# Turning a short chunk of tokens as a full one, with other banks, other engines and one store in place of four, in a masked attention kernel

## The chip, the cores and the metric

The kernel runs on one core of one Trainium2 chip. The metric is device time in microseconds (us) for one execution; the median of three runs is quoted. All data are float32. The core has TensorE (PE, with its weight loads shown as PEld), VectorE (DVE), ScalarE (ACT), GpSimd (POOL) and SyncE (SP), which issues transfers. TensorE writes its results to PSUM, here eight banks of 128 partitions by 512 float32; VectorE and ScalarE empty them.

## The reference

The input x has 8 batches of 512 features by 1024 tokens, cond_2048 is a mask of 0 and 1 for every token, Wq and Wo are 512 by 512.

```python
xt = transpose(x, (0, 2, 1))
q = xt @ Wq.T                                  # 8 heads of 64
scores = scale * einsum('bhqd,bhkd->bhqk', qh, qh)
logits = (scores * cmask + (1 - cmask) * NEG) * rmask
attn = softmax(logits, axis=-1)
ctx = einsum('bhqk,bhkd->bhqd', attn, qh)      # values are the queries too
x + transpose(ctx @ Wo.T, (0, 2, 1))
```

Queries, keys and values are the same projection. A masked key has no weight. A masked query has equal logits everywhere, so its context is the mean over all tokens, and all masked queries of a batch share one result.

## The kernel before, in words

About half the tokens are masked, so the kernel computes with the kept tokens alone, padded to a fixed number NK of 544 columns, of which the last stands for the masked queries and holds the mean token. It finds the kept tokens' places, writes the tokens row by row to a table in DRAM (`xd`), gathers the kept rows, and works on those. If a batch had more kept tokens than fit, or a denominator came out too small, other paths would run; in the execution profiled here they don't.

The 544 columns are five chunks: four of 128 and a short one of 32 (`sizes`, `LAST`, `END`). Heads go in pairs of 64 + 64 rows, so a batch is four pairs, and `pairs` is the list of all 32. For each pair the main loop in `late` goes over five steps (k = 0 to 4, in the order short chunk, then the four full ones), and each step computes the scores of one chunk (`scores`, L687 and L709; the exponentials on ScalarE at L695 and L712). Around the scores the loop does the work that `slots_of` has put into that step: the weighted sums of the pair before (`go_on_attend`, `end_attend`, L751), the values and their lengths of the next pair (`turn_values`, `copy_values`, `lengths_of`, `bias_of`), the projection of the pair after that (`project`, L601), and in some pairs the tokens of the next batch and the output products of the batch before. The order of instructions on each engine is exactly the order in which these functions are called; there is no scheduler.

The parts that the change touches:

- `collect` (L553) turns one chunk of gathered tokens (`xin`, tokens by features) into features by tokens: four turns by TensorE into one PSUM bank, then one copy into `xc`. A full chunk, and all chunks of batch 0, use a transpose (L560). The short chunk of later batches multiplies by the first 32 columns of the identity (L562). Its `xin` holds 128 gathered rows.
- `put_mean` (L569) makes the mean column. Its product shares a bank with the output of the short chunk and with one chunk of the values; VectorE copies it out at L585.
- `bank` hands out PSUM banks. The tag "t" has two banks, "a" has two, and the remaining four belong to the scores. The "a" banks hold the running weighted sums of a pair, from the end of its last step until `end_attend` in step 2 of the next pair (copied out by ScalarE at L778).
- In the third pair of a batch (`new` in `slots_of`), step 3 calls `collect` for five chunks, then `lengths_of`, two of the seven half products of the output (`product`, L968: the output projection is done with seven products of half size in place of eight), and the projections for the first pair of the next batch. Batch 0 does its stage in a branch of its own (`late` in `slots_of`).
- `lengths_of` (L642) squares the values (ScalarE, L646), sums them by head (VectorE, L648) and takes their maximum (L655); TensorE turns it (L658) for a bound on the scores.
- `end_output` (L1040) finishes the output of the last batch: a product with the last pair, added to partial sums by VectorE (L1050, L1057), then stored into the table `od` in DRAM. The short chunk has its 512 features in four groups of 32 partitions, and is stored by four transfers, two from SP and two from ACT (L1060). `fetch_last` (L1090) then gathers eight times from `od`; the first gather waits for chunk 0's and the short chunk's stores. `finish_tokens` (L1119 to L1121) turns the gathered rows, adds x and stores the result.

Of the kernel before, what the change touches and what calls it, by code (L numbers as in the profile page):

```python
# [12 lines left out]
AF = mybir.ActivationFunctionType  # L13
ALU = mybir.AluOpType
# [292 lines left out]
def attention_of_kept_tokens(ctx, tc, n, x, mask, wq, wo, out, ident, wqT, woT, verdict, flag):  # L307


    nc = tc.nc  # L310
    B, D, T = x.shape
    P = 128
# [16 lines left out]
    sizes, places = [], []  # L329
# [40 lines left out]
    def bank(name, tag="t"):  # L370
        if shared["all"]:
            shared["n"] += 1
            tag = "ta"[shared["n"] % 2]
        return ps.tile([P, NB], F32, tag=tag, name=name, bufs=2)
# [3 lines left out]
    xs, xbars, xmeans, xds, xins, xcs, parts, searches = {}, {}, {}, {}, {}, {}, {}, {}  # L378
# [172 lines left out]
        xins[b].append(xin)  # L551

    def collect(b, i, copy=None, tag="t"):  # L553
        n = sizes[i]
        xin = xins[b][i]
        pt = bank(f"xc_{b}_{i}", tag)
        for d in range(ND):
            to, cols = pt[:, d * n : (d + 1) * n], slice(d * P, (d + 1) * P)
            if n == P or b == 0:
                nc.tensor.transpose(to, xin[:n, cols], ident[:n, :n])  # L560
            else:
                nc.tensor.matmul(to, xin[:, cols], ident[:, :n], start=True, stop=True)  # L562
        m = min(n, NK - 1 - i * P)
        (copy or nc.scalar.copy)(
            xcs[b][:, :, i * P : i * P + m],
            pt[:, : ND * n].rearrange("p (d n) -> p d n", d=ND)[:, :, :m],
        )
# [22 lines left out]
    qTs, vs, tops, biases = {}, {}, {}, {}  # L590
# [48 lines left out]
        turn_values(pair)  # L639
        copy_values(pair)  # L640

    def lengths_of(pair):  # L642

        nm = "%d_%d" % pair
        sq = sb.tile([P, NC, P], F32, tag="sq", name=f"sq_{nm}", bufs=1)
        nc.scalar.activation(sq, vs[pair], AF.Square)  # L646
        lengths = sb.tile([P, 2 * NC], F32, tag="len", name=f"len_{nm}")
        nc.vector.tensor_reduce(  # L648
            lengths,
            sq.rearrange("p c (h d) -> p (c h) d", h=2),  # L650
            axis=AX.X,
            op=ALU.add,
        )
        tops[pair] = sb.tile([P, 1], F32, tag="top", name=f"top_{nm}")
        nc.vector.tensor_reduce(tops[pair], lengths, axis=AX.X, op=ALU.max)  # L655
# [218 lines left out]
    ods, gs, xrs = {}, {}, {}  # L874
# [68 lines left out]
            else:  # L943
                nc.vector.tensor_tensor(to, late_[:, upper], both["s", 2][:, j, :], ALU.subtract)

    def product(b, i):

        def tokens(j, m):
            cols = slice(m * P, (m + 1) * P)
            if i in (3, 5, 6, 7):  # L950
                return both["s", {3: 4, 5: 1, 6: 2, 7: 3}[i]][:, j, cols]
            first = 2 * P if i == 4 else 0
            cols = slice(first + m * P, first + (m + 1) * P)
            return cTs[b, j if i == 1 else 2 + j][:, cols]

        def features(j):
            if i == 1:
                return woT[:, j, 0:HALF]
            if i == 2:
                return woT[:, 2 + j, 0:HALF]  # L960
            if i == 3:
                return woT[:, 2 + j, HALF:D]
            return both["t", {4: 4, 5: 1, 6: 2, 7: 3}[i]][:, j, :]

        po = bank(f"po_{b}_{i}")
        for m in range(2):
            for j in range(2):
                nc.tensor.matmul(  # L968
                    po[:, m * HALF : (m + 1) * HALF],
                    tokens(j, m),  # L970
                    features(j),
                    start=(j == 0),
                    stop=(j == 1),
                )

        def new(name):
            t = both[name] = sb.tile([P, D], F32, tag="oc", name=f"{name}_{b}", bufs=LAST)
            return t

        def store(t, row, col):  # L980
            rows = slice(END + row * 2 * P, END + (row + 1) * 2 * P)
            nc.gpsimd.dma_start(  # L982
                ods[b][rows, col * HALF : (col + 1) * HALF].rearrange("(m p) c -> p m c", p=P),
                t.rearrange("p (m c) -> p m c", m=2),
            )

        add = nc.vector.tensor_tensor
        if i == 1:
            ods[b] = dr.tile([NK, D], F32, tag="od", name=f"od_{b}")
            nc.scalar.copy(new("c11"), po)  # L990
        elif i == 6:
            add(new("c12"), po, both["c11"], ALU.add)  # L992
        elif i == 7:
            add(new("c21"), po, both["c12"], ALU.add)
        elif i == 5:
            add(new("c22"), po, both["c21"], ALU.add)
            add(both["c12"], po, both["c12"], ALU.add)
            store(both["c22"], 1, 1)
        elif i == 2:
            add(both["c11"], po, both["c11"], ALU.add)  # L1000
            store(both["c11"], 0, 0)
        elif i == 3:
            add(both["c12"], po, both["c12"], ALU.add)
            store(both["c12"], 0, 1)
        else:
            add(both["c21"], both["c21"], po, ALU.subtract)  # L1006
            store(both["c21"], 1, 0)
# [32 lines left out]
    def end_output(b, i):  # L1040
        n = sizes[i]
        parts = P // n
        w = D // parts
        if i == 0:
            ods[b] = dr.tile([NK, D], F32, tag="od", name=f"od_{b}")
        po = bank(f"po_{b}_{i}")
        add_product(b, i, ND - 1, po, True, True)
        oc = new_rows(b, i, w)
        if parts == 1:
            nc.vector.tensor_tensor(  # L1050
                oc.rearrange("p (d a f) -> p a d f", d=ND, a=A),
                po.rearrange("p (a d f) -> p a d f", d=ND, a=A),
                partials[i].rearrange("p (a d f) -> p a d f", d=ND, a=A),
                ALU.add,
            )
        else:
            nc.vector.tensor_tensor(oc[:, :w], po[:, :w], partials[i][:, :w], ALU.add)  # L1057
        for k in range(parts):
            queue = nc.scalar if k % 2 else nc.sync
            queue.dma_start(ods[b][places[i], k * w : (k + 1) * w], oc[k * n : (k + 1) * n, :w])  # L1060

    def in_blocks(t):
        return t.rearrange("(k f) (a n) -> a f k n", f=Q, a=A)
# [71 lines left out]
    def slots_of(p):  # L1135

        b, pr = pairs[p]
        todo = [[] for _ in range(NC)]
        before = pairs[p - 1] if 0 < p < len(pairs) - 1 else None
        behind = pairs[p + 1] if p + 1 < len(pairs) else None  # L1140
        ahead = pairs[p + 2] if p + 2 < len(pairs) else None

        def do(k, f, *args):
            todo[k].append(lambda: f(*args))
# [3 lines left out]
        by_vector = nc.vector.tensor_copy  # L1148
# [36 lines left out]
        halves = ()  # L1185
# [5 lines left out]
        if not new:  # L1191
            if halves and pr == 1:
                leads[p] = [lambda: product(b - 1, 1)]
                halves = halves[1:]
# [6 lines left out]
        if p == 0:  # L1201
            do(0, project, behind, 1)
            do(1, values, behind)
            do(1, lengths_of, behind)
            do(1, project, ahead, 0)
            do(2, project, ahead, 1)
            do(3, bias_of, behind)
        elif late:
            do(1, values, behind)
            do(2, lengths_of, behind)  # L1210
            do(2, end_attend, before)
            do(2, put_mean, b + 1)
            do(2, collect, b + 1, 0)
            do(3, bias_of, behind)
            do(3, collect, b + 1, 1, by_vector, "a")
            do(3, collect, b + 1, 2, None, "a")
            do(4, collect, b + 1, 3)
            do(4, collect, b + 1, 4)
            for hf in range(2):
                do(4, project, ahead, hf, None, "a")  # L1220
        elif new:
            do(1, short_with_values if halves else mean_with_values)
            do(2, end_attend, before)
            do(3, collect, b + 1, 0, by_vector)
            do(3, collect, b + 1, 1, by_vector)
            do(3, collect, b + 1, 2, by_vector, "a")
            do(3, collect, b + 1, 3, None, "a")
            do(3, collect, b + 1, 4, by_vector)
            do(3, lengths_of, behind)
            for i in halves:  # L1230
                do(3, product, b - 1, i)
            for i in due:
                do(3, output, b - 1, i)
            do(3, project_with_top, 0)
            do(3, project, ahead, 1, None, "a")
        elif ahead:
            do(1, project_with_values)
            do(2, lengths_of, behind)
            do(2, end_attend, before)
            if pr == 1 and b + 1 == B and in_halves:  # L1240
                for k, i in ((2, 1), (2, 6), (3, 7), (3, 5), (4, 2), (4, 3), (4, 4)):
                    do(k, product, b - 1, i)
            do(3, project_with_top, 1, "a" if halves and pr == 1 else "t")
        elif behind:
            do(1, values, behind)
            do(2, lengths_of, behind)
            do(2, end_attend, before)
            do(3, bias_of, behind)
        if p == ND - 1:
# [428 lines left out]
```

## Time and profile before

| | |
|---|---|
| median of three runs | 630.98 us (630.52 to 632.31) |
| the profiled execution | 632.33 us, of which 630.5 us lie between its first and last instruction (the span) |
| busy in the span | PE 597.7, DVE 411.2, ACT 367.0, POOL 223.5 us |
| turns of full chunks, L560 | 128 of 128x128, 17.1 us busy |
| turns of short chunks, L562 | 56 records, 6.8 us busy |
| moved by DMA | 118.02 MB, 187 GB/s in the mean |

The rows of the groups read as: source line, engine, operation, the tile written and the tiles read, shapes, count; then busy time and, where given, the idle time before them with what ended it. A row of the timeline begins with the start in us from the start of the span and the length in us; equal instructions that follow each other are merged into one row with their count. A full-precision matmul stands as two records, a transpose as one. Records overlap, as matmuls are pipelined, so the time that a group holds TensorE is best taken from its start to the start of the next group. A wait's row reads: who waited, for whom, us in total, how often, the longest.

### The profile page before, as it was taken

How to read it: one execution, taken by the hardware profiler on the slowest of the kernel's cores; microseconds unless marked ns; L12 is line 12 of the kernel's file. 1: busy time of each engine (PE TensorE's matmuls, PEld its weight loads, DVE VectorE, ACT ScalarE, POOL GpSimd, SP SyncE). 2: the span in 40 equal slices, each digit the busy share in tenths (PEclk: the TensorE clock that was granted, in tenths of full speed). 3: DMA queues.
4: the chain of work that ended last, by engine and by line, in shares of the span. 5: the costliest groups of instructions: out<-in, count | busy, mean ns of one | idle time of the engine just before them, and what ended most of it. 6: DMA issues, size and time to landing. Idle time of an engine off the chain costs nothing. (4 is left out here: it accounts for less than half of the span.)

```text
span 630.5 us, 16440 instructions
## 1 busy us (share of the span) xinstructions
PE 597.7 (95%) x6298; PEld 416.8 (66%) x6298; DVE 411.2 (65%) x1139; ACT 367.0 (58%) x983; POOL 223.5 (35%) x317
## 2 busy tenths in 40 slices
PE   4799999999999999999999999999999999999963
PEld 3666676677667766777667766777667766765432
DVE  6539767556567767777577767777568735854542
ACT  4256758754766567754776477753775467536400
POOL 6530403232075304731164304830274305337031
PEclk7699999999999999999999999999999999999985
DMA  7565444354488668987698678978695654878557
GB/s 230 181 232 143 143 161 112 107 207 157 150 189 220 215 220 202 193 246 238 192 186 224 211 222 188 204 228 254 183 188 148 171 182 95 172 264 138 114 174 206
DMA packets 95025, 118.02 MB, mean 187 GB/s; under 512 B 11959, under 2 KB 61815, under 8 KB 94942
## 3 DMA queue, kind: packets, MB, share of 16 engines
q1 hardware_dynamic: 74078, 75.17, 39.9%
q0 software_dynamic: 16544, 39.63, 27.1%
q10 hardware_dynamic: 4320, 2.13, 1.2%
q8 instruction: 50, 0.82, 0.5%
q14 instruction: 33, 0.27, 0.2%
HBM read 74.19 MB, written 42.70 MB: 185 GB/s over the span
## 5 line engine op out<-in xcount | busy, mean ns | idle before, releaser
L695 ACT ACTIVATE e<-s,bias 128x544 f32<-128x544 f32 x256 | 180.4, 709 | 70.6 <-PE s L687 67.7
L687 PE MATMUL s<-qT 64*64 64x272 f32 x2048 | 148.6, 396 | 1.2 <-ACT e L695 1.1
L601 PE MATMUL pq<-xc,wqT 128*128 128x272 f32 x512 | 130.8, 400 | 0.0
L751 PE MATMUL av<-e,v 64*64 64x272 f32 x1920 | 129.6, 390 | 0.0
L601 PEld LDWEIGHTS pq<-xc,wqT 128*128 128x128 f32 x512 | 93.8, 190 | 30.4 <-issue 10.3
L687 PEld LDWEIGHTS s<-qT 64*64 64x64 f32 x2048 | 75.0, 132 | 47.4 <-issue 13.3
L751 PEld LDWEIGHTS av<-e,v 64*64 64x64 f32 x1920 | 76.1, 133 | 36.1 <-issue 0.6
L1104 POOL DMA_INDIRECT g<-od,block_origin x56 | 90.4, 1614 | 26.5 <-issue 12.8
L611 ACT COPY qT<-pq 128x272 f32<-128x272 f32 x64 | 24.5, 383 | 105.5 <-PE pq L658 64.4
L982 POOL DMA_DIRECT2D od<-c x28 | 21.1, 754 | 165.3 <-DVE c L1006 97.9
L1074 DVE STREAM_TRANSPOSE xr<-g 128x512 f32<-128x512 f32 x56 | 57.0, 1100 | 0.0
L648 DVE TENSOR_REDUCE len<-sq 128x10 f32<-128x640 f32 x32 | 25.7, 802 | 41.0 <-ACT sq L646 41.0
L695 ACT ACTIVATION_READ_ACCUMULATOR e<-s,bias 128x1 f32 x256 | 50.3, 197 | 0.0
L1101 POOL COPY step<-e 1x1 f32<-1x1 f32 x77 | 26.5, 344 | 55.0 <-ACT e L695 54.7
L545 POOL DMA_INDIRECT xin<-xd,source x40 | 39.5, 989 | 16.2 <-DMA woT<-in_L_cond_Wq_dram 6.0
L968 PE MATMUL po<-t,st 128*128 128x256 f32 x168 | 37.9, 380 | 0.3 <-DVE c L992 0.3
L533 DVE TENSOR_SCALAR_CACHE_REDUCE junk<-rank,key 128x1024 f32<-128x1024 f32 (+4 forms) x35 | 34.9, 998 | 4.9 <-DMA rank<-ranks 4.9
L667 DVE TENSOR_REDUCE m<-pq 128x1 f32<-128x128 f32 x28 | 8.2, 292 | 45.6 <-ACT qT L613 35.5
L475 DVE STREAM_TRANSPOSE xt<-x 128x1024 f32<-128x1024 f32 x28 | 34.7, 1241 | 1.7 <-DMA xd<-xt 1.2
L968 PEld LDWEIGHTS po<-t,st 128*128 128x128 f32 x168 | 31.8, 190 | 5.3 <-DVE c L992 0.7
L494 ACT ACTIVATE junka<-x 128x512 f32<-128x512 f32 x48 | 30.2, 630 | 1.1
L904 POOL DMA_DIRECT2D od<-ol x28 | 14.0, 509 | 45.5 <-ACT v L635 45.4
(210 smaller groups left out, 852.8 us busy)
## 6 DMA issues: line engine op xcount, KB each, us to landing
xd<-xt SPq DMA_DIRECT2D x120, 128.0 KB
x<-in_x_dram SPq DMA_DIRECT2D x56, 256.0 KB
g<-xd SPq DMA_DIRECT2D x56, 256.0 KB
out_dram<-xr SPq DMA_DIRECT2D x28, 512.0 KB
rb<-row SPq DMA_DIRECT2D x60, 160.0 KB
od<-c POOLq DMA_DIRECT2D x28, 256.0 KB, 6.1
rank<-ranks SPq DMA_DIRECT2D x6, 512.0 KB
x<-in_x_dram POOLq DMA_DIRECT2D x8, 256.0 KB, 3.8
```

The lines of the kernel that those rows point to most:

```text
L475: nc.vector.transpose(xt.rearrange("p k (d f) -> p k d f", d=ND), xs[b][r][:, :, at : at + n].rearrange("p d (k t) -> p k d t", t=Q),)
L494: nc.scalar.activation(junk, xs[b][r][:, d, :], AF.Copy, accum_out=xbars[b][:, d, r : r + 1])
L533: nc.vector.tensor_scalar(junk[:, :n], rank[:, i * P :], key[:, col], 0.0, ALU.is_le, ALU.add, accum_out=found[:, col])
L545: nc.gpsimd.indirect_dma_start(out=xin[:n, :], out_offset=None, in_=xds[b], in_offset=bass.IndirectOffsetOnAxis(ap=searches[b][2][:n, i : ...
L601: nc.tensor.matmul(pq[:, :KH], wqT[:, d, pr * P : (pr + 1) * P], xcs[b][:, d, cols], start=(d == 0), stop=(d == ND - 1),)
L687: nc.tensor.matmul(ss[h][r * DK : (r + 1) * DK, hf, :KH], qT[heads[h], c * P + r * DK : c * P + (r + 1) * DK], qT[heads[h], queries[hf]], ...
L695: nc.scalar.activation(e[:, :, h, :], ss[h][:, :, :KH], AF.Exp, bias=bias, scale=SCALE, accum_out=sums[pair[1] % 2][:, h, c : c + 1],)
L751: nc.tensor.matmul(avs[pair][hf][head, :KH], v[keys, c, head], e[keys, hf, h, :], start=(c == 0 and not crossed), stop=(c == LAST - 1 and ...
L968: nc.tensor.matmul(po[:, m * HALF : (m + 1) * HALF], tokens(j, m), features(j), start=(j == 0), stop=(j == 1),)
L1074: nc.vector.transpose(xr.rearrange("p (d a) (t i) -> p a d t i", a=A, i=NT)[..., i], gs[b, i].rearrange("p (a d f) -> p a d f", a=A, f=Q),)
L1101: nc.gpsimd.tensor_copy(step, es[pair, c][0:1, 0, 0, 0:1])
L1104: nc.gpsimd.indirect_dma_start(out=gs[b, i], out_offset=None, in_=ods[b], in_offset=bass.IndirectOffsetOnAxis(ap=block_origin[:, b, i : i ...
```

## The change

The short chunk of every batch but the first is turned as a chunk of 128 rows, by the same transposes as the full ones; the copy still takes only its first 31 columns. In the third pair's step 3 chunk 1 moves from "t" to "a", chunk 3 from "a" to "t"; ScalarE copies chunks 2 and 4 (before: chunk 3), VectorE 0, 1 and 3 (before: 0, 1, 2 and 4). The first of the two half products there goes to an "a" bank. For the last pair of all, VectorE squares the values. In `end_output` the short chunk's rows leave by one transfer on ACT's queue with a destination of four groups by 32 rows.

```diff
     def collect(b, i, copy=None, tag="t"):
-        n = sizes[i]
+        n = sizes[i] if b == 0 else P
         xin = xins[b][i]
         pt = bank(f"xc_{b}_{i}", tag)
         for d in range(ND):
-            to, cols = pt[:, d * n : (d + 1) * n], slice(d * P, (d + 1) * P)
-            if n == P or b == 0:
-                nc.tensor.transpose(to, xin[:n, cols], ident[:n, :n])
-            else:
-                nc.tensor.matmul(to, xin[:, cols], ident[:, :n], start=True, stop=True)
+            nc.tensor.transpose(
+                pt[:, d * n : (d + 1) * n], xin[:n, d * P : (d + 1) * P], ident[:n, :n]
+            )
...
-    def lengths_of(pair):
+    def lengths_of(pair, by_scalar=True):
...
-        nc.scalar.activation(sq, vs[pair], AF.Square)
+        if by_scalar:
+            nc.scalar.activation(sq, vs[pair], AF.Square)
+        else:
+            nc.vector.tensor_tensor(sq, vs[pair], vs[pair], ALU.mult)
...
-    def product(b, i):
+    def product(b, i, tag="t"):
...
-        po = bank(f"po_{b}_{i}")
+        po = bank(f"po_{b}_{i}", tag)
...
-        for k in range(parts):
-            queue = nc.scalar if k % 2 else nc.sync
-            queue.dma_start(ods[b][places[i], k * w : (k + 1) * w], oc[k * n : (k + 1) * n, :w])
+        queue = nc.sync if parts == 1 else nc.scalar
+        queue.dma_start(
+            ods[b][places[i], :].rearrange("n (k w) -> k n w", k=parts),
+            oc[:, :w],
+        )
...
             do(3, collect, b + 1, 0, by_vector)
-            do(3, collect, b + 1, 1, by_vector)
-            do(3, collect, b + 1, 2, by_vector, "a")
-            do(3, collect, b + 1, 3, None, "a")
-            do(3, collect, b + 1, 4, by_vector)
+            do(3, collect, b + 1, 1, by_vector, "a")
+            do(3, collect, b + 1, 2, None, "a")
+            do(3, collect, b + 1, 3, by_vector)
+            do(3, collect, b + 1, 4)
             do(3, lengths_of, behind)
-            for i in halves:
-                do(3, product, b - 1, i)
+            for i, tag in zip(halves, "at"):
+                do(3, product, b - 1, i, tag)
...
             do(1, values, behind)
-            do(2, lengths_of, behind)
+            do(2, lengths_of, behind, False)
             do(2, end_attend, before)
```

## The prediction

> **What bounds the kernel now.** I read the page first, then busy time by stage, then the waits, and last the order of time in the stages that the diff touches.
>
> ```profile
> PE 597.7 (95%) x6298; PEld 416.8 (66%) x6298; DVE 411.2 (65%) x1139; ACT 367.0 (58%) x983; POOL 223.5 (35%) x317
> PEclk7699999999999999999999999999999999999985
> q1 hardware_dynamic: 74078, 75.17, 39.9%
> q10 hardware_dynamic: 4320, 2.13, 1.2%
> ```
>
> TensorE (PE) is busy for 95% of the span, and its granted clock stands at 9 (90% or more) from the third slice to the last but two. A busy PE could still be waiting inside its pipeline, so the next view is busy time by batch (a batch takes about 70 us) and for the end.
>
> ```profile
> 130.00:200.00 70.00, 69.96 (x781) 50.15 (x780) 46.66 (x136) 45.27 (x123) 26.86 (x36) 1.00 0.63 166
> 411.00:481.00 70.00, 69.83 (x779) 49.79 (x778) 50.91 (x140) 45.27 (x123) 26.57 (x36) 1.00 0.79 210
> 604.00:630.00 26.00, 11.17 (x39) 6.78 (x39) 8.98 (x19) 0.00 (x0) 7.64 (x8) 0.61 0.68 206
> ```
>
> The columns are stretch, length, then busy time of PE, PEld, DVE, ACT and POOL, granted clock, DMA share, GB/s. In a batch PE has 0.04 to 0.17 us of idle time in 70; VectorE (DVE) and ScalarE (ACT) have 19 to 25 us each. Only in the last 26 us is PE idle, and there the gathers rule. So what PE no longer issues between 60 and 604 us should come off the end, one for one.
>
> ```profile
> ACT e L695 <- PE s L687: 67.7, 81, 2.3
> PEld xc L560 <- DVE xc L585: 1.5, 5, 0.4
> ```
>
> The first row is ACT waiting for PE, 81 times; the second a wait of PE itself: five times the turning of gathered tokens (L560) stands until VectorE has written the mean column (L585) out of the bank that the turn wants.
>
> **The change part by part.** Each batch from the second on has one stage, in its predecessor's third pair, where five chunks of tokens are turned. Here is PE in two of them, a stage without that wait and one with it:
>
> ```profile
> 142.81 1.97 PE L560 MATMUL xc<-ident,xin 128*128 128x128 f32 x16
> 144.61 0.98 PE L562 MATMUL xc<-ident,xin 128*128 128x32 f32 x8
> 145.42 1.97 PE L968 MATMUL po<-woT,cT 128*128 128x256 f32 x8
> ...
> 423.66 2.32 PE L560 MATMUL xc<-ident,xin 128*128 128x128 f32 x16
> 425.82 0.98 PE L562 MATMUL xc<-ident,xin 128*128 128x32 f32 x8
> 426.63 1.97 PE L968 MATMUL po<-woT,cT 128*128 128x256 f32 x8
> 428.44 1.89 PE L968 MATMUL po<-woT,st 128*128 128x256 f32 x8
> 430.17 1.08 PE L601 MATMUL pq<-xc,wqT 128*128 128x272 f32 x4
> ```
>
> *Short chunk turned as 128 rows.* Four full-precision products stand as eight records and hold PE from 425.82 to 426.63, 0.81 us. After the change they are four turns like those of L560: 16 of them take 144.61 - 142.81 = 1.80 us, 0.11 each, so 0.44 us. The eight products behind the short chunk take 428.44 - 426.63 = 1.81 us, the next eight 430.17 - 428.44 = 1.73: another 0.08, which I expect to go with the switch of kind. Gain 0.37 + 0.08 = 0.45 us. It occurs in seven stages (56 records of L562 by 8): 3.15 us. All on PE, so all on the path. If the 0.08 stays, 2.6.
>
> *Turns and half products in other banks.* Chunks 1 and 2 now take the two "a" banks, chunks 3 and 4 the "t" banks. The wait with L585 makes the 16 turns last 425.82 - 423.66 = 2.16 us in place of 1.80: 0.36. The waits' view has 1.5 us in five; 0.36 three times and 0.17 twice is 1.42, from the starts of these groups. What is late next must be looked for on the two engines that empty the banks:
>
> ```profile
> 423.71 0.68 DVE L585 TENSOR_SCALAR xc<-po 32x4 f32<-32x4 f32 x4
> 424.43 2.01 DVE L564 COPY xc<-xc 128x512 f32<-128x512 f32 x3
> 426.83 0.29 DVE L564 COPY xc<-xc 128x124 f32<-128x124 f32 x1 [0.40 <-PE xc L562]
> 427.27 0.82 DVE L648 TENSOR_REDUCE len<-sq 128x10 f32<-128x640 f32 x1 [0.15 <-ACT sq L646]
> ...
> 422.85 0.67 ACT L778 COPY cT<-av 128x272 f32<-128x272 f32 x2 [0.31 <-PE av L751]
> 426.02 0.58 ACT L564 COPY xc<-xc 128x512 f32<-128x512 f32 x1 [0.72 <-PE xc L560]
> 426.50 0.74 ACT L646 ACTIVATE sq<-v 128x640 f32<-128x640 f32 x1
> ```
>
> The "a" banks are free once L778 has copied the contexts, at 423.52; chunk 1 would start at 423.66 + 0.49 = 424.15: no wait. Chunk 3 takes the mean's bank, free at 423.71 + 0.68 = 424.39, and starts at about 425.0: 0.6 us of cover. Chunk 4 takes chunk 0's bank, copied by 425.12, and starts at 425.46. The first half product (now "a") takes chunk 1's bank: the second of the copies from 424.43 ends near 425.7, the product starts at 423.66 + 20 x 0.11 + 0.06 = 425.9. That cover, 0.2 us, is the thinnest. The second half product takes chunk 4's bank, which ACT has copied by 426.4, and starts at 427.6. I cost the waits at nothing and the gain at 1.42 us.
>
> One copy of 128x512 and the short copy change places between VectorE and ScalarE:
>
> ```profile
> L564 ACT COPY xc<-xc x13: 262/585/586, 28.0 to 496.3; 128x512 f32<-128x512 f32 x11, 128x124 f32<-128x124 f32 x2
> L870 DVE TENSOR_TENSOR cT<-cT,rb 128x544 f32<-128x544 f32 x31 | 22.5, 726 | 1.2
> ```
>
> ScalarE gets the short copy, 0.26 us (its shortest L564), six times; VectorE loses it. The squares behind it end near 427.0, lengths and their maximum near 428.2, and PE turns that maximum only after the projection that starts at 430.17 (about 429.4 then): covered by over 1 us.
>
> *Last batch's lengths squared by VectorE.* This happens once, for the last pair.
>
> ```profile
> 569.82 0.82 DVE L648 TENSOR_REDUCE len<-sq 128x10 f32<-128x640 f32 x1 [4.32 <-ACT sq L646]
> 570.89 0.32 PE L658 MATMUL top<-ident,top 128*128 128x128 f32 x1 [0.16 <-DVE top L655]
> 569.05 0.73 ACT L646 ACTIVATE sq<-v 128x640 f32<-128x640 f32 x1
> 569.86 0.67 ACT L778 COPY cT<-av 128x272 f32<-128x272 f32 x2
> 570.42 0.73 ACT L695 ACTIVATE e<-s,bias 128x544 f32<-128x544 f32 x1
> ```
>
> VectorE sits idle for 4.32 us before the lengths, so the product (128x640 at the rate of L870: about 0.85 us) is covered; PE's wait of 0.16 goes, and ScalarE's exponentials (L695) can start up to 0.73 earlier, but their scores come from PE at about 570.3. I take 0.1 us; bounds 0 and 0.4.
>
> *Short rows stored by one transfer.* This is in the final chain: the first gather waits for these stores.
>
> ```profile
> 604.29 0.34 SPq L1060 DMA_DIRECT2D od<-oc  x1
> 604.73 0.85 SPq L1060 DMA_DIRECT2D od<-ol  x2
> 604.49 0.83 ACTq L1060 DMA_DIRECT2D od<-ol  x2
> 607.97 1.00 POOL L1090 DMA_INDIRECT g<-od,origin  x1 [26.11 <-DVE worst L1568]
> od<-c POOLq DMA_DIRECT2D x28, 256.0 KB, 6.1
> od<-ol POOLq DMA_DIRECT2D x28, 16.0 KB, 2.7
> 616.30 1.96 PE L1119 MATMUL o<-ident,g 128*128 128x128 f32 x8 [0.93 <-DMA g<-od,origin]
> ```
>
> The last of four issues ends at 604.73 + 0.85 = 605.58; a single one on ACT's queue would end near 604.9, 0.7 us earlier. It carries 64 KB in place of 16: by the two rows of stores into od, (6.1 - 2.7) x 48 / 240 = 0.7 us longer to land, net 0. By the hardware queue's rate (75.17 MB in 39.9% of 16 engines and 630.5 us, 299 GB/s) it is 0.16 longer, net 0.5 gained. SP's queue loses two issues and ACT's one; SP's next store isn't helped by it, as VectorE makes it ready at about 605.7, and ACT's queue holds nothing else until the first output. I take 0, since those two rows go to the same tensor, and keep 0.5 for the range; down to -0.5 if the larger transfer lands later than that.
>
> [...]
>
> **Sum.** 3.15 + 1.42 + 0.1 + 0 = 4.67 us. The profiled execution has 632.33 us, 630.5 of span and 1.83 around it; it stands 1.35 above the median of the runs, 630.98. The sum gives 627.7 for such an execution, and 630.98 - 4.67 = 626.3 for the median.
>
> **The rivals.**
> A, a new wait at the first half product: its cover is 0.2 us. Were VectorE's copies 0.45 us later than drawn (one more item of L585's size in front), PE would stand 0.25 us in six stages: 1.5 back, 627.8. For it: VectorE is busy throughout that stretch. Against: nothing is added in front of those copies.
> B, the change of banks doesn't do what it says: the wait for the mean's bank moves to chunk 3 rather than goes, 626.3 + 1.4 = 627.7. Against: 0.6 us of cover.
> C, hidden anyway: another engine sets the pace and takes the time back, about 630.5. Against: 69.83 of 70 us busy, and ACT's waits for PE.
> D, slower: turns don't keep the clock up. The turns of L1119 at the end, under a granted clock of 0.61, run at (1.96 - 0.42) / 7 = 0.22 us each, twice 0.11. If 20 turns in a row pull the clock to half in each stage, 20 x 0.11 x 6 + 8 x 0.11 = 14 us come on top: 640. It decides only if the clock falls in at least three of the seven stages. Against: 16 turns in a row from 142.81 run in 1.80 us, with clock 1.00 in the stretch.
>
> [...]
>
> **How the numbers follow.** Forecast as summed (625.4 to 627.3, with the tail from -0.5 to 0.5, the squares to 0.4 and the 0.08 open) 0.70; A 0.10; B 0.06; C 0.08; D and other losses 0.06. The range 625.3 to 628.6 takes in A and B; C and D stay out. A measurement of this kernel tells 0.3% (1.9 us) from no change: faster is below 629.1, so the forecast, A and B with 0.86; within, C with 0.08; slower 0.06.
>
> **What would show it.** After the change: no record of 128x32, four more full turns in each stage, 20 turns followed within 2.3 us by the half product in all six; no PE wait for L585; the first half product without a wait for the copy; the last pair's top without the 0.16; the first gather 3.5 to 4.2 us after its short store is issued (now 607.97 - 604.49 = 3.48, for the first of four). A copy as PE's releaser at L968 would prove A; a PEclk digit below 9 in mid span D; a PE busy share that falls with the span unchanged, C.

## The result and the profile after

The changed kernel takes 627.11 us (median of six runs, 626.5 to 629.31), the kernel before 631.37 us beside it (630.52 to 632.66). The ratio is 0.9938, with a 95% interval of 0.9917 to 0.9958. Two later comparisons, on other occasions, gave 0.9928 (0.9898 to 0.9958) and 0.9924 (0.9908 to 0.994; 626.27 against 631.66 us). By these medians the kernel is faster by 4.2 to 5.4 us. The forecast was 626.3, or 4.67 us less.

The profiled execution of the changed kernel has 627.36 us, with a span of 625.6. Line numbers move by a few: the turns are now L558, their copies L562, the mean's copy L583, the half products L969, the projection L599. These are the busy line and the clock of its page:

```profile
PE 596.1 (95%) x6270; PEld 415.4 (66%) x6270; DVE 410.0 (66%) x1134; ACT 367.8 (59%) x988; POOL 223.0 (36%) x317
PEclk9999999999999999999999999999999999999985
```

PE has 28 records fewer, and is as full as before. Next, the order of time on PE in the stage that the prediction showed at 423.66 us, and the copies of that stage on VectorE and ScalarE:

```profile
421.05 2.40 PE L558 MATMUL xc<-ident,xin 128*128 128x128 f32 x20
423.29 1.89 PE L969 MATMUL po<-woT,cT 128*128 128x256 f32 x8
425.02 1.89 PE L969 MATMUL po<-woT,st 128*128 128x256 f32 x8
426.75 2.00 PE L599 MATMUL pq<-xc,wqT 128*128 128x272 f32 x8
...
420.92 0.68 DVE L583 TENSOR_SCALAR xc<-po 32x4 f32<-32x4 f32 x4
421.75 2.00 DVE L562 COPY xc<-xc 128x512 f32<-128x512 f32 x3
422.62 0.59 ACT L562 COPY xc<-xc 128x512 f32<-128x512 f32 x1
423.49 0.26 ACT L562 COPY xc<-xc 128x124 f32<-128x124 f32 x1 [0.29 <-PE xc L558]
```

Twenty turns stand in one row. From the first to the first half product it is 423.29 - 421.05 = 2.24 us, where before it was 426.63 - 423.66 = 2.97. The eight half products behind take 1.73 in place of 1.81. From the first turn to the projection the stage has 5.70 us in place of 6.51. In all six stages of the third pairs the 2.24 comes out to within 2 ns; before, the six had 2.62, 2.78, 2.79, 2.98, 2.97 and 2.97. With the 0.08 behind each this gives 0.46 + 0.63 + 0.63 + 0.82 + 0.81 + 0.81, and the earliest stage, where only the short chunk changes kind, gives 0.46 more: 4.6 us. Of this, 1.41 is the wait for the mean's copy as it stood in the one profile of before; that wait has two sizes, as the experiments show.

The whole times agree with that only by way of two other steps. The weighing of the last chunk (L733, now L734) stands in every pair, and serves as a mark: in the kernel before, and then in the one after.

```profile
184.16 0.64 PE L733 MATMUL av<-el,v 64*64 64x272 f32 x8
204.62 0.64 PE L733 MATMUL av<-el,v 64*64 64x272 f32 x8
577.91 0.40 PE L733 MATMUL av<-el,v 64*64 64x272 f32 x2
...
409.09 1.99 PE L968 MATMUL po<-t,st 128*128 128x256 f32 x8 [0.26 <-DVE c L992]
```

```profile
183.23 0.64 PE L734 MATMUL av<-el,v 64*64 64x272 f32 x8
204.61 0.64 PE L734 MATMUL av<-el,v 64*64 64x272 f32 x8
573.68 0.40 PE L734 MATMUL av<-el,v 64*64 64x272 f32 x2
...
188.12 0.23 DVE L863 TENSOR_TENSOR rb<-rb 128x64 f32<-128x64 f32 x1 [4.08 <-DMA rb<-row]
198.13 1.99 PE L969 MATMUL po<-t,st 128*128 128x256 f32 x8 [0.65 <-DVE c L993]
```

At the last mark the changed kernel is 577.91 - 573.68 = 4.23 us ahead (0.6 more comes behind it, where the gathers rule). But at 183 us it was 0.93 ahead, and one pair later only 0.01: 0.92 us was lost where the diff touches nothing. VectorE waited 4.08 us for rows of reciprocals that come back through DRAM (2.73 us in the kernel before), then worked without a pause up to the combination of half products (L993), and PE stood for that. The execution of before has a small case of the same wait at 409.09, worth about 0.5 us, which the one after lacks. So 4.6 + 0.5 - 0.9 = 4.2. In a second profile of the changed kernel neither wait shows, and its mark stands 577.91 - 572.15 = 5.76 us ahead: 4.6 of the stages, 0.5, and 0.6 gained in the start-up, which differs from run to run.

```profile
572.15 0.40 PE L734 MATMUL av<-el,v 64*64 64x272 f32 x2
```

Its waits of PE, between the start-up and the end, are few, and none is for a copy out of a bank of turns. The one with the longest sum (us in total, times, longest):

```profile
PE s L688 <- ACT e L696: 1.4, 4, 0.6
```

### The profile page after: what moved, and what is told of

Read it like the earlier page. It is cut to its first block, busy times and chain, and to the rows that moved or that the text cites. A ratio compares the mean times of both kernels' runs of the same rounds, so it can differ in the third digit from the quotient of the medians.

```text
span 625.6 us, 16380 instructions
## 1 busy us (share of the span) xinstructions
PE 596.1 (95%) x6270; PEld 415.4 (66%) x6270; DVE 410.0 (66%) x1134; ACT 367.8 (59%) x988; POOL 223.0 (36%) x317
## 5 line engine op out<-in xcount | busy, mean ns | idle before, releaser
L599 PE MATMUL pq<-xc,wqT 128*128 128x272 f32 x512 | 130.7, 399 | 0.0
L599 PEld LDWEIGHTS pq<-xc,wqT 128*128 128x128 f32 x512 | 93.8, 190 | 30.4 <-issue 10.7
L688 PEld LDWEIGHTS s<-qT 64*64 64x64 f32 x2048 | 75.0, 132 | 47.5 <-issue 13.1
L1077 DVE STREAM_TRANSPOSE xr<-g 128x512 f32<-128x512 f32 x56 | 57.0, 1100 | 0.0
L649 DVE TENSOR_REDUCE len<-sq 128x10 f32<-128x640 f32 x32 | 25.6, 802 | 38.2 <-ACT sq L645 38.2
L969 PE MATMUL po<-t,st 128*128 128x256 f32 x168 | 37.9, 380 | 0.7 <-DVE c L993 0.7
L969 PEld LDWEIGHTS po<-t,st 128*128 128x128 f32 x168 | 31.7, 190 | 5.8 <-DVE c L993 1.1
```

The costliest lines, as they stand in the source:

```text
L599: nc.tensor.matmul(pq[:, :KH], wqT[:, d, pr * P : (pr + 1) * P], xcs[b][:, d, cols], start=(d == 0), stop=(d == ND - 1),)
L688: nc.tensor.matmul(ss[h][r * DK : (r + 1) * DK, hf, :KH], qT[heads[h], c * P + r * DK : c * P + (r + 1) * DK], qT[heads[h], queries[hf]], ...
L969: nc.tensor.matmul(po[:, m * HALF : (m + 1) * HALF], tokens(j, m), features(j), start=(j == 0), stop=(j == 1),)
L1077: nc.vector.transpose(xr.rearrange("p (d a) (t i) -> p a d t i", a=A, i=NT)[..., i], gs[b, i].rearrange("p (a d f) -> p a d f", a=A, f=Q),)
```

## The experiments

The first four runs each make one part of the change in the kernel before. In that session the kernel before took 641 to 654 us, and in the four profiles PE stands for 1.1 to 4 us at waits outside the diff several times in an execution, so whole times can't tell a third of a per cent there, and these runs are read by their stages.

**The short chunk's turns alone.**

```diff
-        n = sizes[i]
+        n = sizes[i] if b == 0 else P
...
-            to, cols = pt[:, d * n : (d + 1) * n], slice(d * P, (d + 1) * P)
-            if n == P or b == 0:
-                nc.tensor.transpose(to, xin[:n, cols], ident[:n, :n])
-            else:
-                nc.tensor.matmul(to, xin[:, cols], ident[:, :n], start=True, stop=True)
+            nc.tensor.transpose(
+                pt[:, d * n : (d + 1) * n], xin[:n, d * P : (d + 1) * P], ident[:n, :n]
+            )
```

> The kernel before with one part of the change: the short chunk turned as 128 rows, in the old banks. Theory 1 (the forecast's: PE is the path, every saved nanosecond of it comes off the end): each of seven stages loses 0.37 us of products and 0.08 us of the half products behind them, so 3.1 us less than before, ratio 0.995; the wait of the turns for the mean's copy stays, about 0.36 us in some stages. If only the products' own time counts, 2.6 us, ratio 0.996. Rival (the gain of the whole change is the wait for the bank, and a shorter turn only makes that or a later wait longer): under 1 us, ratio 0.999, with a copy as PE's releaser at the first half product. Rival on the clock (more turns in a row lower it): not faster, granted clock under 0.95 in the middle of the span.

The ratio was 0.9829 (0.9729 to 0.993), which is more than this edit can give and no measure of it. On PE, the first of the six stages and the fifth:

```profile
146.47 2.40 PE L558 MATMUL xc<-ident,xin 128*128 128x128 f32 x20
148.71 1.89 PE L966 MATMUL po<-woT,cT 128*128 128x256 f32 x8
...
431.96 2.58 PE L558 MATMUL xc<-ident,xin 128*128 128x128 f32 x20
434.37 1.89 PE L966 MATMUL po<-woT,cT 128*128 128x256 f32 x8
436.10 1.89 PE L966 MATMUL po<-woT,st 128*128 128x256 f32 x8
```

The stage without the wait takes 2.24 us, 0.375 less than the 2.62 with products; the eight half products take 436.10 - 434.37 = 1.73. So 0.45 us a stage, as forecast, and no copy stands ahead of the half product. The wait for the mean's copy stays: five stages have 2.41 to 2.42, as the second above (434.37 - 431.96). But it is 0.17 to 0.18 us in all five, not the 0.36 that was expected in some. VectorE ends the mean's copy either 0.55 or 0.74 us after the first turn, and stages of one and the same kernel show both. With the old banks the first makes PE stand for 0.17 us, the second for 0.36: in the profile of before twice and three times, with the store alone and with the squares alone three times and twice, here and in the run with 32 rows five times and never. What decides between the two, and whether the quicker turns have a part in it, isn't shown.

**The banks alone.**

```diff
-    def product(b, i):
+    def product(b, i, tag="t"):
...
-        po = bank(f"po_{b}_{i}")
+        po = bank(f"po_{b}_{i}", tag)
...
-            do(3, collect, b + 1, 1, by_vector)
-            do(3, collect, b + 1, 2, by_vector, "a")
-            do(3, collect, b + 1, 3, None, "a")
-            do(3, collect, b + 1, 4, by_vector)
+            do(3, collect, b + 1, 1, by_vector, "a")
+            do(3, collect, b + 1, 2, None, "a")
+            do(3, collect, b + 1, 3, by_vector)
+            do(3, collect, b + 1, 4)
...
-            for i in halves:
-                do(3, product, b - 1, i)
+            for i, tag in zip(halves, "at"):
+                do(3, product, b - 1, i, tag)
```

> The kernel before with one part of the change: the chunks' turns, their copies and the half products in the other banks; the short chunk still by products of 32 columns. Theory 1: the wait for the mean's copy goes from six stages, 1.4 us less than before, ratio 0.998; the 16 turns of 128 rows take 1.75 to 1.8 us in all of them, and no new wait stands at the third chunk or at the first half product, whose cover is 0.2 + 0.37 us here. Rival (the wait moves on): ratio 1.000, and a copy stands as PE's releaser in these stages. If the two parts hang together (the banks pay only with the short turns), the sum of this run and of the run with the turns alone falls short of 4.3 us by over 1.

The ratio was 1.0008 (0.9973 to 1.0043), no answer at this size. The fifth stage:

```profile
431.15 1.97 PE L560 MATMUL xc<-ident,xin 128*128 128x128 f32 x16
432.96 0.98 PE L562 MATMUL xc<-ident,xin 128*128 128x32 f32 x8
433.77 1.97 PE L968 MATMUL po<-woT,cT 128*128 128x256 f32 x8
435.58 1.89 PE L968 MATMUL po<-woT,st 128*128 128x256 f32 x8
```

All six stages take 2.61 to 2.62 us up to the half product: the wait is gone from all five that had it, and none came in its place. Against the profile of before that is 0.17 + 0.17 + 0.36 + 0.355 + 0.355 = 1.41 us, where the forecast had 1.42, read in that same profile. In the four profiles with old banks that the experiments add, the waits sum up to 0.85 to 1.23 us (0.89 in the run with the turns alone), so an execution gains that much or 1.41. The 0.08 stays here (435.58 - 433.77 = 1.81), so the banks don't remove it. The two parts add: 0.375 + 0.36 is the 2.97 - 2.24 that the fifth stage of the profile before lost with the whole change. (In the run with the turns alone this stage is 2.97 - 2.41 = 0.56 us shorter: 0.375 by the turns, and 0.18 as its wait was of the smaller size.)

**The store alone.**

```diff
-        for k in range(parts):
-            queue = nc.scalar if k % 2 else nc.sync
-            queue.dma_start(ods[b][places[i], k * w : (k + 1) * w], oc[k * n : (k + 1) * n, :w])
+        queue = nc.sync if parts == 1 else nc.scalar
+        queue.dma_start(
+            ods[b][places[i], :].rearrange("n (k w) -> k n w", k=parts), oc[:, :w]
+        )
```

> The kernel before with one part of the change: the last short rows stored by one transfer on ACT's queue in place of four on two queues. Theory 1: nothing, within 0.5 us either way (ratio 0.999 to 1.001): the first gather starts 3.4 us after the store is issued, as 3.48 after the first of four. In the changed kernel this issue took 1.1 us for 128 rows of 512 bytes, and its rows went out on four DMA engines in 0.84 us; both should be seen again. Rival (the tail gained from the store): the first gather 0.5 us earlier against the first issue, 2.9 us.

The ratio was 0.9973 (0.9931 to 1.0016). What counts is the first gather against the first issue of these rows:

```profile
619.06 1.11 ACTq L1059 DMA_DIRECT2D od<-ol  x1
622.49 0.99 POOL L1092 DMA_INDIRECT g<-od,origin  x1 [24.91 <-DVE worst L1570]
```

It is 3.43 us here. Over all profiles of this case, the five kernels with four stores have 3.47 or 3.48, the eight with this single one 3.40 to 3.44. The change of the store is worth 0.05 us. What comes behind the gathers varies more than that: from the first long store to the end it is 26.2 us before, 25.6 after, and 25.0 and 25.2 in the two runs above, which have the old store.

**The squares alone.**

```diff
-    def lengths_of(pair):
+    def lengths_of(pair, by_scalar=True):
...
-        nc.scalar.activation(sq, vs[pair], AF.Square)
+        if by_scalar:
+            nc.scalar.activation(sq, vs[pair], AF.Square)
+        else:
+            nc.vector.tensor_tensor(sq, vs[pair], vs[pair], ALU.mult)
...
-            do(2, lengths_of, behind)
+            do(2, lengths_of, behind, False)
```

> The kernel before with one part of the change: the last pair's squares by VectorE. The forecast had 0.1 us less. From the two traces I now expect 0: the maximum is ready over 1 us before PE turns it, the wait of 0.16 us in front of that turn goes, but PE then stands the same time at the scores behind it, which wait for ScalarE's exponentials. Ratio 1.000. Rival (ScalarE's 0.73 us are on the path): 0.4 us or more less, and no wait at those scores.

The ratio was 0.9995 (0.996 to 1.003). The last pair:

```profile
587.57 0.83 DVE L649 TENSOR_TENSOR sq<-v 128x640 f32<-128x640 f32 x1 [1.96 <-ACT v L636]
...
589.28 0.16 DVE L658 TENSOR_REDUCE top<-len 128x1 f32<-128x10 f32 x1
...
590.29 0.67 ACT L781 COPY cT<-av 128x272 f32<-128x272 f32 x2 [1.02 <-PE av L754]
590.76 0.32 PE L661 MATMUL top<-ident,top 128*128 128x128 f32 x1
...
591.72 1.83 PE L690 MATMUL s<-qT 64*64 64x272 f32 x16 [0.64 <-ACT e L698]
```

The product takes 0.83 us and the maximum is ready 1.3 us before PE turns it. But ScalarE, freed of its 0.73 us, stands 1.02 us until PE has the contexts that it copies next (L781), so its exponentials begin no earlier, and PE now waits at the scores for a bank that they empty. In the kernel before the squares lay in a gap of ScalarE. The profiles before and after agree: this pair takes 12.31 us from mark to mark in both, and the copy of the contexts begins 2.26 us behind the start of their sums in both.

The next four runs change the changed kernel, or try another form; the kernel before took 632.62 us in that session, in a single run.

**VectorE's copies later.**

```diff
+        def hold_vector():
+            held = sb.tile([P, D], F32, tag="held", name=f"held_{p}", bufs=1)
+            nc.vector.tensor_copy(held, woT[:, 0, :])
...
+            do(3, hold_vector)
             do(3, collect, b + 1, 0, by_vector)
```

> The changed kernel with one more VectorE copy of 128x512 (0.69 us, into a tile that nobody reads) ahead of the chunks' copies in each of the six stages. In the changed kernel the copy of chunk 1 ends 0.2 us before the first half product that takes its bank, and the copy of chunk 0 about 0.4 us before chunk 4's turns. Theory 1 (cover is what the trace draws, PE is the path): chunk 4's turns stand 0.2 to 0.3 us and the first half product stands until 0.4 to 0.5 us later than now, with VectorE's copy as releaser, so the 20 turns and the next product take 2.65 to 2.75 us in place of 2.24, 2.5 to 3 us in all. Rival (the banks have more cover than drawn, or another engine sets the pace): the stages stay at 2.24 us.

```profile
423.04 2.44 PE L558 MATMUL xc<-ident,xin 128*128 128x128 f32 x20
423.62 0.43 DVE L1155 COPY held<-woT 128x512 f32<-128x512 f32 x1
424.08 1.88 DVE L562 COPY xc<-xc 128x512 f32<-128x512 f32 x3
425.42 1.99 PE L969 MATMUL po<-woT,cT 128*128 128x256 f32 x8
427.25 1.89 PE L969 MATMUL po<-woT,st 128*128 128x256 f32 x8
```

The added copy, between two places of SBUF, held VectorE for 424.08 - 423.62 = 0.46 us, not the 0.69 that I had taken from copies out of PSUM. In the changed kernel VectorE stood idle for a part of that time, waiting for the first turns. So its copies of the chunks now begin 424.08 - 423.04 = 1.04 us behind the first turn, where without the added copy it was 421.75 - 421.05 = 0.70: 0.34 later. The half product begins 2.38 us behind the first turn, 0.15 later than in the changed kernel, with VectorE's copy as releaser. So 0.34 - 0.15 = 0.2 us were absorbed, and that is the cover that the prediction read off the trace. Another 0.10 us is lost behind: the eight half products take 427.25 - 425.42 = 1.83 in place of 1.73. Five stages show this, 0.25 in all; the first, where VectorE was ahead, has 2.24. The marks on PE fall back by 0.25 in each of the five, one for one. The expectation of 2.65 to 2.75 was too high, as it took the added copy for 0.69 us, and all of it as delay.

**Every turn twice.**

```diff
-        for d in range(ND):
+        for d in [*range(ND)] * (1 if b == 0 else 2):
```

> The changed kernel with every turn of gathered tokens from the second batch on made twice (the second writes the same values over the first). Theory 1: 20 more turns cost 20 x 0.109 = 2.18 us a stage, so 4.42 us in place of 2.24, the granted clock stays at 1.00 in the middle of the span, and the whole is 7 x 2.18 = 15.3 us longer than the changed kernel. Rival (turns pull the clock down once there are enough in a row): over 0.11 us for a turn late in the stage, 5 us or more a stage, and a clock digit below 9.

642.5 us. The last stage on PE, and one stage by the view of stretches (stretch, length, busy PE, PEld, DVE, ACT and POOL, granted clock, DMA share, GB/s):

```profile
503.09 4.59 PE L558 MATMUL xc<-ident,xin 128*128 128x128 f32 x40
507.51 1.89 PE L969 MATMUL po<-woT,cT 128*128 128x256 f32 x8
...
287.10:291.60 4.50, 4.50 (x45) 4.46 (x42) 2.62 (x7) 2.09 (x5) 1.14 (x2) 1.00 0.30 87
```

4.42 us, 2.18 more for 20 turns, so 0.109 each in the 40th as in the first, at a granted clock of 1.00. The six stages add 13.1 us and the earliest one 1.7 of its 2.2, 14.8 in all. The span is 640.8 - 625.6 = 15.2 us longer, where theory 1 had 15.3; the last few tenths are other waits, which differ from run to run. The granted clock stands at 1.00 from 26 to 619 us, so in none of the stages did the 40 turns lower it. These are turns between other products; what clock turns alone would be granted isn't shown.

**Two stores of 64 rows.**

```diff
-        queue = nc.sync if parts == 1 else nc.scalar
-        queue.dma_start(
-            ods[b][places[i], :].rearrange("n (k w) -> k n w", k=parts),
-            oc[:, :w],
-        )
+        if parts == 1:
+            nc.sync.dma_start(ods[b][places[i], :], oc[:, :w])
+        else:
+            to = ods[b][places[i], :].rearrange("n (k w) -> k n w", k=parts)
+            for queue, ks in ((nc.scalar, slice(0, parts // 2)), (nc.sync, slice(parts // 2, parts))):
+                queue.dma_start(to[ks], oc[ks.start * n : ks.stop * n, :w])
```

> The changed kernel with the last short rows stored by two transfers of 64 rows, one on ACT's queue and one on SP's, in place of one of 128 rows. If a transfer's rows are spread by the count of its slowest dimension (4 there, 2 here), each goes out on two DMA engines, 32 rows each, as slowly as the single one (0.84 us), and only the shorter issue is gained: about 0.55 us in place of 1.11, the first gather 0.3 us earlier against the first issue (3.1 in place of 3.4 us). If they are spread over all engines, each takes a quarter of the time or less and the first gather comes 0.8 us earlier or more (2.6 us).

```profile
600.16 1.11 ACTq L1064 DMA_DIRECT2D od<-ol  x1
600.40 0.59 SPq L1064 DMA_DIRECT2D od<-ol  x1
604.33 1.00 POOL L1094 DMA_INDIRECT g<-od,origin  x1 [25.55 <-DVE one L1576]
```

Neither expectation: the first gather is 4.17 us behind the first issue, 0.8 later than with one store. ACT's issue took 1.11 us for 64 rows as for 128, SP's 0.59. In the trace's packets ACT's 64 rows run from 601.53 to 602.41 us, and SP's, issued 0.24 us later, don't begin before 602.41. The semaphore of each transfer was updated once ahead of its data and twice behind. For the single store of the changed kernel it is once ahead and four times behind, and its 128 packets of 28 ns in the mean run from 601.60 to 602.44, 0.84 us; each of the four stores of the kernel before has sixteen updates. So ACT's 64 rows took 0.88 us where the single store's 128 took 0.84, half the rate, and the packets of the second transfer came behind those of the first. The first expectation had the rate of each transfer right, but not that the two would run one behind the other. The engines themselves aren't named in the trace. That the single store's rows went out on four is an estimate, by 128 x 28 ns / 0.84 us = 4.3 packets at a time beside its four updates; for two in each transfer here there is the half rate alone, beside the two updates.

**The short chunk turned as 32 rows.** This is the form that the first batch has, put in the kernel before, with the old banks:

```diff
-            if n == P or b == 0:
+            if True:
                 nc.tensor.transpose(to, xin[:n, cols], ident[:n, :n])
-            else:
-                nc.tensor.matmul(to, xin[:, cols], ident[:, :n], start=True, stop=True)
```

> The kernel before with the short chunk turned as 32 rows (what the first batch does) in place of products, in the old banks. In the first batch of the kernel before four such turns hold PE for 0.36 us, with 0.09 us more in front of them. Theory (what counts is turn in place of product, not the rows): 0.36 + 0.09 against four turns of 128 rows with 0.44, so a stage without the wait takes 2.23 to 2.27 us, as with 128 rows, and the half products behind lose 0.08 too. Rival (the switch to another tile shape costs more than it did there): 2.4 us or more.

```profile
142.76 2.33 PE L560 MATMUL xc<-ident,xin 128*128 128x128 f32 x20
145.02 1.99 PE L966 MATMUL po<-woT,cT 128*128 128x256 f32 x8
146.85 1.46 PE L966 MATMUL po<-woT,st 128*128 128x256 f32 x6
```

2.26 us to the half product, as expected, and 629.52 us in a single run. But the half products keep a delay: 146.85 - 145.02 = 1.83, even 0.10 over 1.73. So turn in place of product gives 0.36, and of the forms tried the 0.08 behind it goes only with turns of 128 rows. In all these runs the delay lies between the two records of the first half product: 0.22 us from start to start behind turns of 128 rows, 0.30 behind the short products, 0.32 behind turns of 32 rows, and 0.32 too where PE had stood just before, as in the run with the late copies. With both, 128 rows are 0.12 us a stage better than 32.

**The wait outside the diff.** The last runs ask whether the steps at the combination of half products can be removed, by moving VectorE's turning of two finished blocks of rows (L1077, 2.04 us), which stands between the reciprocals' rows and that combination: behind the combination, or ahead of the wait for the rows.

```diff
-        FINISH = {(0, 4): (0, 1), (1, 1): (2, 3), (1, 3): (4, 5), (1, 4): (6, 7)}
+        FINISH = {(0, 4): (0, 1), (1, 3): (2, 3, 4, 5), (1, 4): (6, 7)}
```

> The changed kernel with one more edit: the turning of the two finished blocks of rows (VectorE, 2.04 us) that stands between VectorE's wait for the reciprocals' rows and its combination of half products is put behind that combination. Theory (PE's steps of 0.3 to 2 us in the second pair of a batch come from that wait, and the 2 us of turning in front of the combination is what leaves it no cover): PE's wait for the combination goes, 0.3 to 0.7 us less than the changed kernel in a quiet execution, up to 6 us on a chip with slow transfers, and a narrower spread of the times. Rival (the steps have another origin, or the turning is late for its own stores): the wait stays, or the same time turns up behind it.

```profile
274.38 1.99 PE L969 MATMUL po<-t,st 128*128 128x256 f32 x8 [1.79 <-DVE c L993]
291.36 1.38 PE L558 MATMUL xc<-ident,xin 128*128 128x128 f32 x8 [0.88 <-DVE xc L583]
```

The rival: the 2 us come back one pair later, at the mean's copy (the mark falls back by 1.6 us in five of the six stages), and the wait at the combination stays. At the row of 274.38 VectorE wasn't late: it had stood 4.85 us for the product. The ratio to before is 1.0051 (1.0019 to 1.0084), beside 0.9928 for the changed kernel on the same chip (before: 640.22 us):

> The changed kernel again, beside the next run on the same chip. Theory 1: 4.2 to 4.7 us less than before where the chip's transfers are as quick as in the first profiles (ratio 0.993), with steps of 0.3 to 2 us on top in some pairs of some executions, where VectorE's wait for the rows of reciprocals (read back through DRAM) lets PE stand at the second pair's combination of half products.

```profile
336.46 3.73 PE L969 MATMUL po<-t,st 128*128 128x256 f32 x16
...
341.40 0.69 DVE L993 TENSOR_TENSOR c<-po,c 128x512 f32<-128x512 f32 x1 [3.18 <-PE po L969]
...
342.15 1.13 PE L969 MATMUL po<-t,st 128*128 128x256 f32 x4 [1.96 <-DVE c L993]
```

Here too VectorE wasn't late at all. It stood 3.18 us for the product's completion, whose signal came at 341.3 us, though its last record on PE begins at 338.0; in the quiet profile of before such a signal comes 0.4 us after that start. This is the common case: of the fourteen waits of PE of 1.8 to 2.1 us at this combination, in six profiles, every one has VectorE standing for 2.4 to 4.9 us for PE's signal. VectorE was late itself at three shorter waits alone: 0.65 us (after), 0.26 (before) and 0.38 (every turn twice). What held the signals back stays open: the granted clock is 1.00 at this one, and neither move of the turning could have touched it.

```diff
-        FINISH = {(0, 4): (0, 1), (1, 1): (2, 3), (1, 3): (4, 5), (1, 4): (6, 7)}
+        FINISH = {(0, 4): (0, 1, 2, 3), (1, 3): (4, 5), (1, 4): (6, 7)}
```

> The changed kernel with the turning of two finished blocks of rows (VectorE, 2.04 us) put ahead of VectorE's wait for the reciprocals' rows, where VectorE stands idle for 2.7 to 4.1 us in the profiles, in place of behind it. Theory (part of PE's steps in the second pair come from VectorE being late with the combination): 2 us more of cover there, nothing late in exchange, so 0.65 us less in an execution like the changed kernel's profile and 0 to 1 us less in the median (ratio to before 0.991 to 0.993); where VectorE is already waiting for PE's own signal, nothing changes. Rival (the blocks' rows aren't there yet so early): VectorE waits for their gathers instead, the reciprocals' rows are used later, and the run is slower than the changed kernel, as with the turning put behind.

> The changed kernel, beside the next run on the same chip: 4 to 5 us less than before (ratio 0.993).

Waits of VectorE in the run with the turning ahead (us in total, times, longest):

```profile
DVE xr L1077 <- DMA g<-od,block_origin: 8.0, 5, 3.0
DVE rb L863 <- DMA rb<-row: 3.9, 2, 2.2
```

VectorE's wait for the reciprocals' rows shrinks from 16.5 us in the second profile of the changed kernel to 3.9, and a wait of 8.0 for the blocks' gathers takes its place. PE stands once, 0.4 us, for an operand of the products that VectorE makes late. 626.49 us against 626.27 for the changed kernel: no difference that can be told.

## Why the prediction was right, step by step

*What bounds.* Right. Each saved or added piece of PE in the third pairs moved the marks one for one, in both directions: 0.45 us less a stage with the turns alone, 0.25 more with the late copies, 2.18 more with every turn twice. Rival C, a gain taken back elsewhere, falls.

*The short chunk.* 0.37 + 0.08 a stage was forecast; 0.375 + 0.08 stands in the run with the turns alone. That the 0.08 goes was a guess, without a reason given, and it came right; the run with 32 rows has turns too, and keeps a delay.

*The banks.* That the wait goes and none comes in its place was forecast, and the run with the banks alone shows it. The row of L558 has no wait, so rival B falls. Rival A falls too, but the thinnest cover was drawn rightly: 0.2 us, by the run with the late copies. The size, 1.42 against 1.41, agrees so closely only because both are read against the same profile; other executions with the old banks had 0.85 to 1.23 to lose.

*The squares.* 0.1 was forecast, 0 measured. PE's wait of 0.16 at the maximum went, as said. The step that failed is the worth of ScalarE's earlier exponentials: the prediction looked for what their scores wait for, but the copy of the contexts stands between squares and exponentials, and waits for PE anyway.

*The store.* 0 was forecast with bounds of 0.5 either way; the gather gained 0.05. The 3.5 to 4.2 us that I named for it was a little high, at 3.40. Both terms behind the 0 were off. The prediction let the single issue end near 604.9, 0.4 us after its start; it took 1.11 us, as long as the four together (605.58 - 604.49 = 1.09). And it let the larger transfer land 0.7 us later behind its issue; by the last update of the semaphore it landed 1.43 us behind it, the last of the four 1.47. So the 0 came right by two errors that cancel, which is luck.

*Clock, rival D.* Falls: with every turn twice, forty turns in a row kept a granted clock of 1.00.

*The sum.* 4.67 forecast; 4.60 by the stages, against one profile of before. The comparisons of medians give 4.26, 4.24 and 5.39. In the profiles, differences of this size come from the two sizes of the wait for the mean's copy, from steps at the combination of half products, and from start-up and end, none of which the prediction weighed; which of them moved the medians isn't shown. That the first median came within 0.8 us of 626.3 is therefore in part luck, while the 4.6 of the stages is not.

## What to carry to other kernels

Where one engine is full, read its own records by stage, start to start: a part of the change that saves 0.36 us there comes out exactly, when the whole time can't show it. Look at more than one profile before you price a wait: this one had two sizes. Ahead of moving work off an engine, look at what that engine does next and whether it would wait there anyway. And ahead of turning several transfers into one, look at the outermost count: here a transfer with a count of 4 carried its 128 rows in 0.84 us, and one with a count of 2 needed 0.88 us for 64.

## What the runs showed of the hardware

- A full-precision product with 32 columns took about as much for each of its two records as a turn of 128 (0.112 against 0.109 us from start to start, before), so four of them took nearly twice the time of four turns (0.81 against 0.44 us), and the eight half products behind took 1.81 us, where they took 1.73 behind twenty turns of 128 rows (after).
- A store's issue on ACT's queue took 1.11 us with 64 rows (two stores) and with 128 (after), and 0.36 to 0.44 with 32 (before); two transfers on two queues, each with an outermost count of two, ran one behind the other: the second's first packet began where the first's last one did, at 602.41 us.
- After four of the fourteen waits of PE of 1.8 to 2.1 us the granted clock fell to 0.50 for 3.4 us (once with the turns alone, once with the store alone, twice with the squares alone; waits of 1.86 to 1.97 us). The run with the turns alone, in stretches around such a wait:

```profile
484.00:488.00 4.00, 3.48 (x16) 2.48 (x14) 2.14 (x4) 3.06 (x8) 3.22 (x5) 1.00 0.84 223
...
490.40:497.40 7.00, 7.00 (x53) 4.98 (x55) 2.95 (x7) 1.68 (x5) 0.77 (x1) 0.76 0.12 44
```

With this wait of 1.97 us the pair takes 4.1 us longer than in the profile of before; in pairs with waits of 1.87 and 1.86 us of the same run, and of 1.96 in the changed kernel's repeat, without a fall of the clock, it is 2.3 to 2.4. So the fall costs about 1.7 us on top (3.4 us at half the clock). What decides between the two isn't shown.
